# Three taps of a grouped convolution: summed in the accumulator, or shifted by small DMAs and summed in the next product

## The chip, the cores and the metric

The kernel runs on one core of a Trainium2 chip. The time is that of one execution on the device, in microseconds (us). Of the engines, TensorE multiplies matrices (PE in the profile, its weight loads PEld), VectorE (DVE) and ScalarE (ACT) work on whole tiles and can read the accumulators, GpSimd (POOL) works on tiles in the main on-chip memory, and SyncE (SP) starts DMAs. ScalarE and GpSimd can start DMAs too, each in its own row of instructions.

## The reference, cut to what matters

Two layers run one after the other on an image batch of shape (2, 128, 256, 256) in float32. The first is a group norm and a windowed attention with halo; the change leaves it alone. The second is a group norm and this convolution block, added to its input:

```python
t1 = conv(x, w1, padding=((2, 2), (0, 0)))                 # 128 -> 128 channels, 5 rows
t3 = conv(t1, w3, padding=((1, 1), (0, 0)), groups=128)    # 3 rows, per channel
xp = pad(x, columns by (2, 2))
t2 = stack([xp[..., 0:w], xp[..., 2:w + 2], xp[..., 4:w + 4]], axis=2)
t4 = einsum('nckhw,ckg->nghw', t2, w4[:, :, 0, :])         # 3 taps, 128 -> 8 channels
t5 = t4[:, None] * t3.reshape(n, 16, 8, h, w)
x = x + t5.reshape(n, 128, h, w)
```

`t4` takes each pixel and its neighbours two columns to the left and to the right, multiplies the 128 channels of each with a matrix of 128 x 8, and sums the three. Its 8 channels are then multiplied into 128 channels of `t3`, channel `ch` taking channel `ch % 8` of `t4`.

## The kernel before

The second layer is `convolutions_fast`. It goes over 64 strips `k`, 32 for each image, each of 8 rows of 256 columns, with the 128 channels in the partitions. The instructions of every engine stand in the order in which the Python code gives them (`manual_schedule`), so an engine that waits holds everything behind it.

Per strip, in the order of the code:

- `load_rows1(k + 2)` (L629) starts two loads from SyncE, L636 and L638, two strips ahead.
- `unfold(k)` (L686) makes `t4`. `g` is one accumulator bank of 128 x 512. Its four groups of 32 partitions hold two rows of the strip each, and of the 32 only 8 carry data; the weights are padded with zeros to 32 columns. For each of the three taps there are four matrix products (L692), one for each group, and the three taps are summed in the accumulator by `start=tap == 0, stop=tap == 2`. ScalarE copies the bank to `t4` (L698).
- `first_rows(k)` (L709): ScalarE copies two rows of `t1` from the strip before (L723).
- In strips 1 and 2 a step of a range check (`count_good`), and in strips 2 to 7 steps of the group norm of the second image (`norm.steps`). Some of these are small products whose result goes to bank `b3`, some are small operations on VectorE, among them L119, and one is a square root on ScalarE (L139), with its table load.
- `start_strip(k + 1)` (L666) normalises the next strip: ScalarE copies four rows that overlap (L649), VectorE does the new ones (L651).
- `vertical(k, 2)` (L727) makes the first four rows of the vertical convolution `t1`. The products `a_c`, `a_d`, `a_e`, `a_o` take one bank each, in this order, from a pool of three (`ps_a`, L618). ScalarE copies `a_c` to `both` (L737). VectorE adds `both` to `a_d` (L744, giving `c`), then `c` to `a_e` (L751) and to `a_o` (L757). ScalarE multiplies the rows with the first tap of `w3` (L762).
- `row_sums(k + 1)` (L670): a small ScalarE copy (L677) and two VectorE operations (L678, L682) for the next strip.
- `depthwise(k, 2)` (L764): two VectorE operations, L769.
- `vertical(k, 4)`: the same for the last four rows.
- `spread(k)` (L774): four products (L780) with the constant `sel` spread the 8 channels of `t4` over 128 partitions, one bank each, `b0` to `b3`. Each has 32 partitions of `t4` as its inner dimension; `sel` has a one at row `ch % 8` of each 32.
- `combine` multiplies the four banks with `t3` on VectorE (L789), with `depthwise(k, 4)` between the first two and the last two; `finish(k)` (L794) lets GpSimd start a DMA that adds the layer's input to the strip (L797), and SyncE the store (L798).

The first layer and the fallback function `tile_halo_attention_then_conv`, which does not run on these inputs, are not touched, though the fallback has functions of the same names.

Of the kernel before, what the change touches and what calls it, by code (L numbers as in the profile page):

```python
# [9 lines left out]
F32 = mybir.dt.float32  # L10
# [9 lines left out]
P = 128  # L20
W = 256
# [27 lines left out]
def host_constants():  # L49
    ident = np.eye(P, dtype=np.float32)  # L50
    gavg = np.zeros((P, P), np.float32)
    for g in range(P // 4):
        gavg[4 * g : 4 * g + 4, 4 * g : 4 * g + 4] = 0.25

    kb = np.zeros((HEADS, 32, 6, 10), np.float32)
    for c in range(10):
        kb[:, c, :, c] = 1.0
    for r in range(6):
        kb[:, 10 + r, r, :] = 1.0
    kb[:, 16, :, 6:] = NEG  # L60
    kb[:, 17, :, :4] = NEG
    flag = np.zeros((2, 4 * NPAIR * 4, 2, 4), np.float32)
    flag[0, :, 0] = 1.0
    flag[1, :, 1] = 1.0


    hot = np.zeros((2, HEADS, 16, 2, 64), np.float32)
    for key in range(64):
        j, i = divmod(key, 6)
        for e in range(2):  # L70
            if 0 <= j - 4 * e < 6:
                hot[:, :, j - 4 * e, e, key] = 1.0
            else:
                hot[:, :, 12, e, key] = NEG
            if key < 60:
                hot[:, :, 6 + i, e, key] = 1.0


    keep = np.zeros((2, HEADS, 16, 2, 2), np.float32)
    for i in range(2):  # L80
        keep[:, i::2, 0:12, i, 0] = 1.0
        keep[:, i::2, 12, i, 1] = 1.0

    sel = np.zeros((4, 32, P), np.float32)
    for ch in range(P):
        sel[:, ch % 8, ch] = 1.0
    return {
        "c_ident": ident,
        "c_sel": sel.reshape(P, P),
        "c_gavg": gavg,  # L90
        "c_kb": kb.reshape(P, 60),
        "c_flag": flag.reshape(2, 4 * NPAIR, 32),
        "c_hot": hot.reshape(P, 128),
        "c_keep": keep.reshape(P, 4),
        "c_head": np.stack([(np.arange(P) // DH % 2 == i) for i in range(2)], 1).astype(np.float32),
    }


class Norms:


    def __init__(self, nc, glob, small, gavg, ns):
        self.nc, self.glob, self.small, self.gavg, self.ns = nc, glob, small, gavg, ns
        self.done = {}
# [478 lines left out]
class Weights:  # L583


    def __init__(self, nc, io, glob):
        self.nc, self.io = nc, io
        self.w1 = glob.tile([P, 5, P], F32, tag="w1", name="w1")
        self.w3 = glob.tile([P, 3], F32, tag="w3", name="w3")
        self.w4 = glob.tile([P, 3, 32], F32, tag="w4", name="w4")  # L590
        self.sel = glob.tile([P, P], F32, tag="sel", name="sel")
        self.w1s = glob.tile([P, 6, P], F32, tag="w1s", name="w1s")

# [13 lines left out]
def convolutions_fast(tc, io, x1_d, norm, st_y, out, weights, count_good):  # L607

    nc = tc.nc
    NB, _, H, _ = io["x"].shape  # L610
    NS = H // 8
    with ExitStack() as l1:
        cst = l1.enter_context(tc.tile_pool(name="f_l1c", bufs=1))
        rawp = l1.enter_context(tc.tile_pool(name="f_raw1", bufs=6))
        tp = l1.enter_context(tc.tile_pool(name="f_t1", bufs=2))
        wk = l1.enter_context(tc.tile_pool(name="f_wk1", bufs=2))
# [4 lines left out]
        w1, w3, w4, sel, w1s = weights.w1, weights.w3, weights.w4, weights.sel, weights.w1s  # L621
# [19 lines left out]
        def normalise1(b, s, k, mean, rstd):  # L641
            cur, prev = xn[k % 2], xn[(k + 1) % 2]
            if s == 0:
                nc.gpsimd.memset(cur[:, 0:1, :], 0.0)
                nc.vector.tensor_scalar(
                    cur[:, 1:4, 2 : 2 + W], raws[b, -1][:, 5:8, :], mean, rstd, ALU.subtract, ALU.mult
                )
            else:
                nc.scalar.copy(cur[:, 0:4, :], prev[:, 8:12, :])  # L649
            n = 8 if s + 1 < NS else 5  # L650
            nc.vector.tensor_scalar(  # L651
                cur[:, 4 : 4 + n, 2 : 2 + W], raws[b, s][:, 0:n, :], mean, rstd, ALU.subtract, ALU.mult
            )
            if n < 8:
                nc.gpsimd.memset(cur[:, 4 + n : 12, :], 0.0)

        t1s, sms, dfs = {}, {}, {}

# [5 lines left out]
        def start_strip(k):  # L666
            b, s = divmod(k, NS)
            normalise1(b, s, k, *norm.done[f"y{b}"])
# [17 lines left out]
        def unfold(k):  # L686

            xt = xn[k % 2]
            pg = ps_pj.tile([P, 512], F32, tag="pj", name=f"g_{k}")
            for tap in range(3):  # L690
                for j in range(4):
                    nc.tensor.matmul(  # L692
                        pg[32 * j : 32 * j + 32, :], w4[:, tap, :],
                        xt[:, 2 * j + 1 : 2 * j + 3, 2 * tap : 2 * tap + W],
                        start=tap == 0, stop=tap == 2,
                    )
            t4 = wk.tile([P, 512], F32, tag="t4", name=f"t4_{k}")
            nc.scalar.copy(t4, pg)  # L698
            t3 = wk.tile([P, 8, W], F32, tag="t3", name=f"t3_{k}")
            y = wk.tile([P, 8, W], F32, tag="y", name=f"y_{k}")  # L700
            ts[k] = t4, t3, y
# [7 lines left out]
        def first_rows(k):  # L709

            s = k % NS
            xt = xn[k % 2]

            t1s[k] = t1 = tp.tile([P, 10, W], F32, tag="t1", name=f"t1_{k}")
            if s == 0:
                nc.gpsimd.memset(t1[:, 0:1, :], 0.0)
                top = taps(
                    f"{k}_first", 1,
                    [(w1[:, tap], xt[:, tap - 1 : tap, 2 : 2 + W]) for tap in (2, 3, 4)],
                )  # L720
                nc.scalar.copy(t1[:, 1:2, :], top)
            else:
                nc.scalar.copy(t1[:, 0:2, :], t1s[k - 1][:, 8:10, :])  # L723
            if s + 1 == NS:
                nc.gpsimd.memset(t1[:, 9:10, :], 0.0)
# [48 lines left out]
        def spread(k):  # L774

            t4 = ts[k][0]
            banks = []
            for j in range(4):
                pb = ps_b.tile([P, 512], F32, tag=f"b{j}", name=f"b_{k}_{j}")
                nc.tensor.matmul(  # L780
                    pb, sel[32 * j : 32 * j + 32, :], t4[32 * j : 32 * j + 32, :], start=True, stop=True
                )
                banks.append(pb)
            return banks
# [29 lines left out]
        with tc.manual_schedule(engines=ORDERED):  # L814
            for k in range(2):
                load_rows1(*divmod(k, NS))
            start_strip(0)
            row_sums(0)
            for k in range(NB * NS):
                more = k + 1 < NB * NS  # L820
                if k + 2 < NB * NS:
                    load_rows1(*divmod(k + 2, NS))
                unfold(k)
                first_rows(k)


                if k in (1, 2):
                    count_good[k - 1](ps_b, "b3")
                if k == 2:
                    steps = norm.steps(st_y[NB - 1], ps_b, f"y{NB - 1}", "b3")  # L830
                for _ in range({3: 1, 4: 2, 5: 2, 6: 1, 7: 1}.get(k, 0)):
                    next(steps)
                if more:
                    start_strip(k + 1)

                vertical(k, 2)
                if more:
                    row_sums(k + 1)
                depthwise(k, 2)
                vertical(k, 4)  # L840
                banks = spread(k)
                combine(k, banks, (0, 1))
                if not more:
                    finish_half(k, 0)
                depthwise(k, 4)
                combine(k, banks, (2, 3))
                if more:
                    finish(k)
                else:
                    finish_half(k, 1)  # L850
# [559 lines left out]
def lay_out(inputs):  # L1410

    c = np.ascontiguousarray
    w_qkv = np.asarray(inputs["L0_conv_W_qkv"])
    rel = np.concatenate(
        [np.asarray(inputs["L0_conv_rel_width"]).T, np.asarray(inputs["L0_conv_rel_height"]).T], axis=1
    )
    w4 = np.asarray(inputs["L1_conv_w4"])[:, :, 0, :]
    return {
        "x": c(np.asarray(inputs["x"])),
        "w_qkvT": c(w_qkv.T),  # L1420
        "w_q": c(w_qkv[:P]),
        "w_outT": c(np.asarray(inputs["L0_conv_W_out"]).T),
        "relT": c(np.tile(rel, (HEADS, 1))),
        "w1T": c(np.asarray(inputs["L1_conv_w1"])[:, :, :, 0].transpose(1, 2, 0)),
        "w3": c(np.asarray(inputs["L1_conv_w3"])[:, 0, :, 0]),
        "w4": c(np.tile(w4, (1, 1, P // w4.shape[-1]))),
        "w4g": c(np.pad(w4, ((0, 0), (0, 0), (0, 32 - w4.shape[-1])))),
        **host_constants(),
    }

# [16 lines left out]
```

## Time and profile before

| | |
|---|---|
| median of 3 runs | 3231.89 us (3228.91 to 3233.07) |
| the profiled execution | 3226.79 us |
| its span, as the profile counts | 3224.9 us |
| mean clock granted to TensorE | 0.996 of full speed |
| busy, share of the span | PE 96%, PEld 71%, DVE 81%, ACT 45%, POOL 18% |

Busy shares are means over two layers with different limits. These are the groups of the second layer's instructions that the change touches or that stand beside them, with count, busy time and the mean duration of one, and after the second bar the idle time of the engine just before them and what ended it:

```profile
L706 PE MATMUL a_e<-xm,w1s 128*128 128x512 f32 x512 | 240.7, 591 | 0.0
L762 ACT ACTIVATE t<-t,w 128x1024 f32<-128x1024 f32 x128 | 147.2, 1150 | 689.0 <-DVE t L757 689.0
L769 DVE SCALAR_TENSOR_TENSOR t<-t,w,t 128x1024 f32<-128x1024 f32 x256 | 329.9, 1289 | 7.5 <-ACT t L762 1.3
L797 POOL DMA_DIRECT2D y<-f_x x63 | 71.3, 1131 | 1025.1 <-DVE y L789 960.7
```

Matrix products overlap in time, so their durations do not add up; the distance between their starts says more. A product in float32 appears as two instructions.

### The profile page before, as it was taken

The page shows a single profiled execution, that of the slowest core. Times are in us where ns is not written, and L with a number is a line of the kernel's source. Part 1 is how long each engine was busy: PE and PEld are TensorE (multiplying, and loading weights), DVE is VectorE, ACT ScalarE, POOL GpSimd, SP SyncE. Part 2 cuts the span into 40 slices and gives each one's busy share as a digit, 9 for nine tenths or more (in the row PEclk, how much of TensorE's full clock was granted, in tenths as well). Part 3 has the DMA queues.
Part 4 walks back from the last instruction along what each step waited for, and adds up shares of the span by engine and source line. Part 5 has one row for each costly group of instructions (what it writes and reads, how often), then busy time and mean ns, then how long its engine had stood idle before and what let it go on. Part 6 is the DMA issues. An engine that isn't in the chain of part 4 may idle for free.

```text
span 3224.9 us, 117425 instructions
## 1 busy us (share of the span) xinstructions
PE 3084.4 (96%) x53030; PEld 2282.9 (71%) x53030; DVE 2611.7 (81%) x4152; ACT 1440.3 (45%) x2481; POOL 586.7 (18%) x917
## 2 busy tenths in 40 slices
PE   0799999999999999999999999989999999999998
PEld 0688898899988889988998889834444444444443
DVE  8788888888888777777777777678888898888887
ACT  0455555555555555555555555522332323233322
POOL 2222222222222222222222222100000000000001
PEclk9999999999999999999999999999999999999999
DMA  9443333333333222222222222146677767676775
GB/s 396 148 133 111 122 108 111 110 120 119 107 111 99 81 75 80 85 68 86 80 78 85 68 88 81 40 135 160 187 194 182 185 186 190 178 190 186 194 182 153
DMA packets 125116, 426.42 MB, mean 132 GB/s; under 512 B 9024, under 2 KB 75328, under 8 KB 92096
## 3 DMA queue, kind: packets, MB, share of 16 engines
q1 hardware_dynamic: 115536, 352.76, 32.2%
q0 software_dynamic: 9072, 66.06, 11.3%
q8 instruction: 420, 6.88, 0.9%
q14 instruction: 88, 0.72, 0.1%
HBM read 284.57 MB, written 134.22 MB: 130 GB/s over the span
## 4 chain that ended last, share of the span: by engine, by line
PE 76%; issue 18%; DVE 2%; POOL 2%; DMA 1%; ACT 0%; SPq 0%; POOLq 0%; DVEq 0%; ACTq 0%
PE f_pv L416 15%; PE f_pq L341 8%; PE f_s L451 8%; PE f_o L476 8%; PE f_pk L341 7%; PE f_py L341 7%; PE a_e L706 5%; PE a_o L706 5%; PE f_pa L395 4%; PE f_s L435 4%; PE g L692 3%; PE a_d L740 2%; POOL y L797 1%; PE b L780 1%; PE a_c L706 1%
## 5 line engine op out<-in xcount | busy, mean ns | idle before, releaser
L422 DVE COPY f_vt<-f_pv 64x512 f32<-64x512 f32 x512 | 354.3, 694 | 291.6 <-ACT f_vt L422 291.4
L416 PE MATMUL f_pv<-f_wqkvT,f_xn 128*128 128x128 f32 x4096 | 491.4, 278 | 0.0
L416 PEld LDWEIGHTS f_pv<-f_wqkvT,f_xn 128*128 128x128 f32 x4096 | 466.9, 192 | 8.6
L762 ACT ACTIVATE t<-t,w 128x1024 f32<-128x1024 f32 x128 | 147.2, 1150 | 689.0 <-DVE t L757 689.0
L323 POOL COPY f_xq<-f_xn 128x256 f32<-128x256 f32 x512 | 309.7, 649 | 757.8 <-DVE f_xn L309 757.8
L376 ACT ACTIVATE f_q<-f_pq,f_head 128x512 f32<-128x512 f32 x512 | 309.9, 687 | 304.2 <-PE f_pq L341 304.2
L460 ACT ACTIVATE f_p<-f_s 128x512 f32<-128x512 f32 x512 | 264.3, 603 | 404.1 <-PE f_s L451 404.0
L422 ACT COPY f_vt<-f_pv 64x512 f32<-64x512 f32 x512 | 297.4, 582 | 118.0 <-PE f_pv L416 117.8
L769 DVE SCALAR_TENSOR_TENSOR t<-t,w,t 128x1024 f32<-128x1024 f32 x256 | 329.9, 1289 | 7.5 <-ACT t L762 1.3
L451 PEld LDWEIGHTS f_s<-f_q,f_kt 64*64 64x64 f32 x16384 | 250.6, 135 | 49.3 <-issue 49.3
L341 PE MATMUL f_pq<-f_xn,f_wq_s 128*128 128x192 f32 (+2 forms) x1520 | 277.2, 330 | 3.3 <-DVE f_xn L309 2.6
L451 PE MATMUL f_s<-f_q,f_kt 64*64 64x64 f32 x16384 | 268.2, 220 | 0.0
L476 PE MATMUL f_o<-f_vt,f_p 128*32 128x66 f32 x16384 | 265.3, 223 | 0.9 <-DVE mean_x L125 0.3
L797 POOL DMA_DIRECT2D y<-f_x x63 | 71.3, 1131 | 1025.1 <-DVE y L789 960.7
L476 PEld LDWEIGHTS f_o<-f_vt,f_p 128*32 128x32 f32 x16384 | 243.2, 111 | 10.5 <-DVE f_cf L408 1.0
L341 PE MATMUL f_pk<-f_xn,f_wqkvT 128*128 128x256 f32 x1024 | 245.3, 380 | 0.0
L341 PEld LDWEIGHTS f_pq<-f_xn,f_wq_s 128*128 128x128 f32 x1520 | 232.3, 188 | 17.0 <-issue 4.2
L341 PE MATMUL f_py<-f_ot,f_woT 128*128 128x256 f32 x1024 | 241.8, 378 | 2.3 <-DVE f_ot L494 2.3
L706 PE MATMUL a_e<-xm,w1s 128*128 128x512 f32 x512 | 240.7, 591 | 0.0
L706 PE MATMUL a_o<-xm,w1s 128*128 128x512 f32 x512 | 240.5, 590 | 0.0
L300 POOL COPY f_xn<-f_xn 128x1280 f32<-128x1280 f32 x62 | 86.5, 1395 | 772.1 <-PE f_pv L416 772.1
L510 DVE TENSOR_TENSOR f_x<-f_py,f_raw 128x512 f32<-128x512 f32 x256 | 175.9, 687 | 58.7 <-PE f_py L341 50.7
(126 smaller groups left out, 4612.6 us busy)
## 6 DMA issues: line engine op xcount, KB each, us to landing
f_raw<-in_x SPq DMA_DIRECT2D x62, 1280.0 KB, 7.8
f_sx<-in_x SPq DMA_DIRECT2D x64, 1024.0 KB, 7.3
f_x<-f_x SPq DMA_DIRECT2D x128, 512.0 KB, 3.3
y<-f_x POOLq DMA_DIRECT2D x63, 1024.0 KB, 8.2
out<-y SPq DMA_DIRECT2D x63, 1024.0 KB, 4.9
raw<-f_x SPq DMA_DIRECT2D x64, 640.0 KB, 6.4
raw<-f_x SPq DMA_DIRECT2D x62, 384.0 KB, 6.9
f_raw<-in_x SPq DMA_DIRECT2D x2, 1024.0 KB, 6.9
```

The lines of the kernel that those rows point to most:

```text
L323: nc.gpsimd.tensor_copy(xq[:, t2, half].rearrange("p t r n c e -> p r t (n c) e"), cells[:, :, 16 * half : 16 * half + 16, 1 + t2 : 9 : 4, ...
L341: nc.tensor.matmul(dst[:, 32 * lo : 32 * hi], w, moving[:, lo:hi], start=True, stop=True)
L376: nc.scalar.activation(q[:, c, :, i], pq.rearrange("p (n x) -> p n x", n=NPAIR), AF.Copy, scale=head[:, i : i + 1],)
L416: nc.tensor.matmul(pv[:, P * n : P * n + P], xn[k % 2][:, r, 4 * j + n].rearrange("p c x -> p (c x)"), wvT, start=True, stop=True,)
L422: (nc.vector.tensor_copy if c else nc.scalar.copy)(vt[rows, 4 * j : 4 * j + 4, :, c, 0:32], pv[rows].rearrange("p (n h d) -> p n h d", n=4 ...
L451: nc.tensor.matmul(sc[g][n // 8][64 * c : 64 * c + 64, n % 8].rearrange("p i x -> p (i x)"), keys_k[rows, c, 48 * n : 48 * n + 64], qs[u][ ...
L460: nc.scalar.activation(pts[u][:, g, 8 * half : 8 * half + 8].rearrange("p n i x -> p (n i x)"), sc[g][half].rearrange("p n i x -> p (n i x ...
L476: nc.tensor.matmul(po[32 * h : 32 * h + 32, n - lo], p[:, h // 2, n, h % 2], vt[:, n, h], start=True, stop=True,)
L510: nc.vector.tensor_tensor(x1[:, :, c:W:2], py.rearrange("p (m t) -> p t m", t=4), raws[k][:, r:8:2, c:W:2], ALU.add,)
L706: nc.tensor.matmul(pa[:, : n * W], w, rows, start=i == 0, stop=i == len(terms) - 1)
L762: nc.scalar.activation(t3[:, j : j + 4], t1[:, j : j + 4, :], AF.Copy, scale=w3[:, 0:1])
L769: nc.vector.scalar_tensor_tensor(t3[:, j : j + 4], t1[:, j + tap : j + tap + 4, :], w3[:, tap : tap + 1], t3[:, j : j + 4], ALU.mult, ALU.add,
```

## The change

The three taps of `t4` are no longer summed in the accumulator. One set of weights holds the 8 columns of each of the three taps side by side, 24 of 32, so four products per strip give the contributions of each pixel to all three taps. ScalarE copies the bank to a tile `by_pixel`, and then starts twelve DMAs for each strip, one for each tap and group: 8 partitions, two rows of 254 or 256 columns, moved by -2, 0 or +2 columns into a tile `t4`. There are two such tiles, which take turns and are set to zero once. The products of `spread` sum over the taps, as `sel` now has a one in three places of each 32 rows. The steps of the range check and of the norm, and `start_strip` before `vertical(k, 2)`, change places: `start_strip(k + 1)` and `vertical(k, 2)` come first, the steps follow.

```diff
-    sel = np.zeros((4, 32, P), np.float32)
+    sel = np.zeros((4, 4, 8, P), np.float32)
     for ch in range(P):
-        sel[:, ch % 8, ch] = 1.0
+        sel[:, 0:3, ch % 8, ch] = 1.0
...
-        self.w4 = glob.tile([P, 3, 32], F32, tag="w4", name="w4")
+        self.w4 = glob.tile([P, 32], F32, tag="w4", name="w4")
...
+        shifted = [cst.tile([P, 2, W], F32, tag=f"t4{i}", name=f"t4_{i}") for i in range(2)]
+        for i in range(2):
+            nc.gpsimd.memset(shifted[i], 0.0)
...
             pg = ps_pj.tile([P, 512], F32, tag="pj", name=f"g_{k}")
+            for j in range(4):
+                nc.tensor.matmul(
+                    pg[32 * j : 32 * j + 32, :], w4, xt[:, 2 * j + 1 : 2 * j + 3, 2 : 2 + W],
+                    start=True, stop=True,
+                )
+            by_pixel = wk.tile([P, 2, W], F32, tag="t4", name=f"t4_{k}")
+            nc.scalar.copy(by_pixel.rearrange("p r w -> p (r w)"), pg)
+
+            t4 = shifted[k % 2]
             for tap in range(3):
+                o = 2 * tap - 2
+                lo, hi = max(0, -o), W - max(0, o)
                 for j in range(4):
-                    nc.tensor.matmul(
-                        pg[32 * j : 32 * j + 32, :], w4[:, tap, :],
-                        xt[:, 2 * j + 1 : 2 * j + 3, 2 * tap : 2 * tap + W],
-                        start=tap == 0, stop=tap == 2,
-                    )
-            t4 = wk.tile([P, 512], F32, tag="t4", name=f"t4_{k}")
-            nc.scalar.copy(t4, pg)
+                    rows = slice(32 * j + 8 * tap, 32 * j + 8 * tap + 8)
+                    nc.scalar.dma_start(t4[rows, :, lo:hi], by_pixel[rows, :, lo + o : hi + o])
...
                 nc.tensor.matmul(
-                    pb, sel[32 * j : 32 * j + 32, :], t4[32 * j : 32 * j + 32, :], start=True, stop=True
+                    pb, sel[32 * j : 32 * j + 32, :],
+                    t4[32 * j : 32 * j + 32].rearrange("p r w -> p (r w)"), start=True, stop=True,
                 )
...
                 unfold(k)
                 first_rows(k)
+                if more:
+                    start_strip(k + 1)
+
+                vertical(k, 2)
...
                 for _ in range({3: 1, 4: 2, 5: 2, 6: 1, 7: 1}.get(k, 0)):
                     next(steps)
-                if more:
-                    start_strip(k + 1)
-
-                vertical(k, 2)
                 if more:
                     row_sums(k + 1)
```

The host pads the weights accordingly (`w4.reshape(P, -1)`, 24 columns to 32).

More of the change, by code (lines that the diff above doesn't have):

```diff
@@ L1426, in lay_out @@
         "w4": c(np.tile(w4, (1, 1, P // w4.shape[-1]))),
-        "w4g": c(np.pad(w4, ((0, 0), (0, 0), (0, 32 - w4.shape[-1])))),
+        "w4g": c(np.pad(w4.reshape(P, -1), ((0, 0), (0, 8)))),
         **host_constants(),
```

## The prediction, made before the changed kernel ran

> **What bounds the kernel now.** I read the busy times by stretch first. The change lies wholly in the second layer (from about 2101 us on), so only that stretch counts. Columns after the stretch and its length are busy us with instruction counts of TensorE, its weight loads, VectorE, ScalarE, GpSimd, then granted clock, DMA share and GB/s.
> ```profile
> 2400.00:2600.00 200.00, 200.00 (x796) 91.49 (x792) 177.50 (x201) 61.23 (x95) 13.01 (x12) 1.00 0.71 186
> ```
> TensorE never rests, VectorE is at 89%, ScalarE at 31%. The accumulating load (L797) starts 59 times between 2213.6 and 3200.0 us, so a strip takes 17.0 us. VectorE works 15.1 us of that. Next, the chain of waits in order of time, for one strip (start, length, what):
> ```profile
> 2516.02 2.74 PE g L692 x24
> 2518.75 0.63 PE a_c L706 x2
> 2519.38 0.86 PE a_d L740 x4
> 2520.25 2.58 PE a_e L706 x6
> 2522.82 2.58 PE a_o L706 x6
> ...
> 2532.07 1.07 PE b L780 x8
> ```
> The whole chain of a strip is TensorE. Times below are from the strip's start (2516.02 = 0). Then ScalarE's timeline of the same strip:
> ```profile
> 2516.57 1.15 ACT L762 ACTIVATE t<-t,w 128x1024 f32<-128x1024 f32 x1 [5.53 <-DVE t L757]
> 2518.81 0.58 ACT L698 COPY t<-g 128x512 f32<-128x512 f32 x1 [1.10 <-PE g L692]
> 2519.29 0.62 ACT L723 COPY t<-t 128x512 f32<-128x512 f32 x1
> 2519.81 1.06 ACT L649 COPY xm<-xm 128x1040 f32<-128x1040 f32 x1
> 2520.78 0.37 ACT L737 COPY both<-a_c 128x256 f32<-128x256 f32 x1
> ```
> ScalarE is idle on average, but this row of four copies ends in `both`, which frees the bank that the first product of `a_o` takes: `ps_a` has three banks, `a_c`, `a_d`, `a_e` fill them, and `a_o` takes the first again. `both` ends at 5.13, `a_o` starts at 6.80: slack 1.7 us. That is the place to watch, as the twelve new DMAs are issued by ScalarE ahead of L723, L649 and L737.
>
> What does an issue cost? No DMA is issued by ScalarE in this trace. SyncE's timeline at the start has eight in a row:
> ```profile
> 1.64 0.43 SPq L172 DMA_DIRECT2D f_woT<-in_w_outT  x1
> 2.12 0.43 SPq L172 DMA_DIRECT2D f_hot<-in_c_hot  x1
> 2.59 0.43 SPq L172 DMA_DIRECT2D f_keep<-in_c_keep  x1
> 3.06 0.43 SPq L172 DMA_DIRECT2D f_head<-in_c_head  x1
> ```
> 1 KB (f_head) or 64 KB (f_woT), the spacing is 0.47 us: the price is for the instruction, not its bytes.
>
> Last, what a rest does to TensorE, from its timeline and the stretches around the normalisation step of 2191 us:
> ```profile
> 2191.45 0.38 PE L122 MATMUL pm_y<-mv_y,f_gavg 128*128 128x1 f32 x2 [3.04 <-DVE y L789]
> 2191.69 1.09 PE L706 MATMUL a_c<-sm,w1s 128*128 128x256 f32 x2
> 2192.57 1.06 PE L740 MATMUL a_d<-df,w 128*128 128x256 f32 x2
> ```
> ```profile
> 2193.00:2195.00 2.00, 2.00 (x5) 1.35 (x4) 1.29 (x2) 0.24 (x1) 0.00 (x0) 0.50 0.99 131
> ```
> After 3.04 us of rest the clock was 0.50 (the mean is 0.71 over the two us before and 0.94 over the two after, so some 3.4 us of half clock), and the work from 2191.69 to 2195.62 took 3.93 us where the strip above needs 2.15 for it (0.43 for `a_c`, 0.86 for `a_d`, 0.86 for the first third of `a_e`): 1.8 us lost. Of the three rests of this kind (3.08 us at 2149, 3.04 at 2188, 3.06 at 2210) only this one lowered the clock.
>
> **What the Trainium skill says.** "Perfetto Trace Analysis", section "DMA Instruction — HWDGE (DVE, Sync)": the recorded time of an issue runs until the sequencer is free for its next instruction, data movement not included. So 0.43 us is time in which ScalarE's later instructions wait; SyncE's spacing agrees. "DMA: Bandwidth & Descriptors", section "SWDGE vs HWDGE vs iDMA": a DMA from ScalarE is made by the same hardware as one from SyncE, so I carry SyncE's price over; no run here shows it yet. Same page, "Why a DMA increments its semaphore by 16 and not by 1": a transfer of 8 partitions runs on 8 engines, and the sequencer adds the other 8 increments itself. No trace here shows that form; it speaks for dearer issues, not cheaper. "TensorE: Matmul & The Clock Gate", section "Part 1": the array falls to half clock after an idle window of about 3.4 us and needs as long of work to recover. The trace agrees in kind (clock 0.50, up again after some 3.4 us), but once after 3.04 us already.
>
> **The change, part by part.**
>
> 1. Products `g`: 12 become 4 per strip. Each group of four runs side by side in 0.86 us, so 2.74 becomes 1.02 us: 1.72 us less for TensorE in each strip.
>
> 2. `b` keeps its form and number (1.07 us); only the rows of `sel` fill up. The copy of `g` stays (0.58 us). The two memsets run on GpSimd, 13 us busy in 200, before the first strip: nothing. One load of weights is 32 KB smaller: nothing.
>
> 3. Twelve issues on ScalarE. The first waits for the copy of `g`. That copy stands behind L762 of the strip before (ends at 1.70 in the trace, set by VectorE), so it ends near 2.2, though `g` is done at 1.02. Price of one: SyncE's spacing 0.47 for 128 rows. L514, with 512 rows, is recorded with 0.51, L798, with 128, with 0.34: 0.45 ns for a row, 0.05 us less for 8 to 16 rows. A little back for the increments: I take 0.44. Bounds: 0.33 (about the shortest issue in the trace, with no gap), 0.60 (about L275's median, 0.62). 12 x 0.44 = 5.3 us. From 2.25 they end at 7.55; L723, L649 and `both` follow in 0.52 + 0.97 + 0.37 and some 0.1 of starts, as spaced in the trace: `both` ends at 9.5. Queued behind it on ScalarE are L762, the copy of `sm` and the second `both`, and VectorE's `c`, `df` and L769 wait for these.
>
> 4. TensorE after it: `a_e` ends 4.06 us after `g`, at 5.08, then TensorE rests until 9.53. From the start of `a_o` to the next `g` the chain has 10.1 us (2505.93 to 2516.02 in the strip before). Period 9.53 + 10.1 = 19.6 us. VectorE's round, from the same `both` through `a_o`, L757, L762, `sm`, `df`, two L769, `c`, L751, L757, L762, the copy of `g` and the issues, comes to the same 19.6, so nothing pulls it in.
>
> 5. The rest is now 4.45 us, longer than the three above. I take half clock in two of three strips, at 1.8 us: 1.2 us. Bounds: none, and 1.8 in each. Period 20.8 us, 3.8 more than 17.0; over 63 strips, +239 us.
>
> 6. The landing. `b` starts at 18; the last issue is at 7.5 and small loads at the start landed in 1.9 to 2.4 us. Ten us of slack: nothing. With eight completion semaphores handed round, as the built program shows, the ninth issue of a strip waits for its first to land (3.5 us earlier: landed), and the eighth waits for the strip before's last `raw` load. That one is issued at 14.9 and lands 6.9 us later, at 21.8, which is 1.0 in a strip of 20.8 and before the eighth issue at 5.3. Hidden here, but see the rival of cheap issues.
>
> 7. Normalisation and counting steps, strips 2 to 7. Before, ScalarE's copies of `g` stand 20.2, 19.3, 21.9 and 20.2 us apart from strip 2 to 6: 81.6 against 4 x 17.0, 13.6 us lost, mostly to TensorE waiting for bank b3 until VectorE's L789 of the strip before. Behind `vertical(k, 2)` that bank is long free: gone. In exchange L119 (3.6 us) stands between L757 and L678 on VectorE, and the table load (1.3 us) ahead of the copy of `sm`, both on the round: 5 back. Net -8 us (bounds -14 and +5).
>
> Sum against the profiled execution: 3226.8 + 239 - 8 = 3458. That execution is 5.1 us under the median of the runs (3231.9), so 3463; I say 3460.
>
> **Rivals.**
>
> *The issues hold ScalarE, but the clock stays up* (two of three short rests kept it). Period 19.6: 63 x 2.6 - 8 = +156, 3388 us. At 0.33 us an issue the rest falls to 3.1 us: period 18.3, +74, 3306.
>
> *Dearer issues*: at 0.60 us the hold is 7.2, `a_o` starts at 11.5, the rest is 6.4 us and the clock falls each time: 11.5 + 10.1 + 1.8 = 23.4, 63 x 6.4 - 8 = +395, 3627. The flat 0.47 over all sizes speaks against.
>
> *Not slower*: ScalarE issues cheaply, as nothing in this trace prices its own. It decides from 9.53 - 5.3 + 12 d + 10.1 = 17.0, d = 0.22 us. With d = 0.1 the sum alone gives 15.5, VectorE's 15.1 plus its 0.44 wait for `sm` the same. But then the eighth issue meets part 6's semaphore: the load lands at 21.8, that is 21.8 less the period, and four more issues and the three copies follow, so twice the period is 21.8 + 0.5 + 2.0 + 10.1 = 34.4: 17.2 us, no gain beyond part 7. If the loads move up with the shorter strip and land 1.5 us earlier, 16.5: 63 x -0.5 - 8 = -40 us, 3192. All of SyncE's issues in the trace, at 0.32 or more, speak against.
>
> **How the numbers follow.** The hold with half clock in most strips 0.55 (its own range 3390 to 3530), the hold with full clock or slightly cheaper issues 0.25, dearer issues 0.08, cheap issues 0.12 (0.09 faster, 0.03 about equal). The range 3300 to 3560 leaves out the cheap issues and most of the dear ones. A difference under 0.2% (6.5 us) can't be told from none. Faster 0.09, same 0.03, slower 0.88.
>
> **What would show it.** ScalarE's queue with twelve issues a strip, 0.4 to 0.5 us apart, between the copy of `g` and that of the two rows of `t1` (L723 before); `a_o` waiting for `both` by some 4 us in each strip; a mean clock near 0.94 over stretches of the second layer; VectorE's share down to some 73%; strips 20 to 21 us apart. Wrong if issues stand under 0.2 us apart, if `both` comes before 6 us, or if TensorE waits at `b` for the shifted rows instead.

## The result, and the profile after

| | before | after |
|---|---|---|
| median of the runs | 3230.4 us | 3774.78 us (3768.13 to 3777.88) |
| ratio, 95% interval | | 1.1683 (1.1667 to 1.1699) |
| the profiled execution | 3226.79 us | 3777.88 us |
| its span | 3224.9 us | 3776.1 us |
| strip to strip, mean from 2400 to 3000 us | 16.94 us | 25.58 us |

The changed kernel is 17% slower. The forecast had the direction and the place, but with 3460 us only 42% of the loss, and the time lies above its range.

The busy times of a stretch, columns as in the prediction, and four lines of the page: the shares of the chain that ended last, and three groups with count, busy time, mean ns of one, and the idle time of the engine before them with what ended it.

```profile
2600.00:2800.00 200.00, 135.35 (x406) 60.74 (x405) 119.21 (x135) 40.53 (x64) 8.62 (x8) 0.84 0.50 126
```

```profile
PE 63%; ACTq 13%; DVE 8%; ACT 7%; issue 6%; DMA 2%; POOL 0%; SPq 0%; DVEq 0%; POOLq 0%
...
L715 PE MATMUL a_o<-xm,w1s 128*128 128x512 f32 x512 | 354.7, 830 | 496.1 <-ACT both L746 496.1
...
L753 DVE TENSOR_TENSOR c<-a_d,both 128x512 f32<-128x512 f32 x128 | 88.0, 688 | 391.8 <-ACT both L746 391.8
...
L732 ACT COPY t<-t 128x512 f32<-128x512 f32 x62 | 38.3, 617 | 561.2 <-DMA t<-t 561.2
```

TensorE fell from 200 us busy in 200 to 135, at a clock of 0.84, and VectorE from 177.5 to 119. Of the chain that ended last, 13% is now "ACTq", which is ScalarE's own row of DMA issues; before, it was 0%. `a_o` waited 496 us for `both`. The 561 us in front of L732 are put down to a DMA, but nothing waits there for a landing: the chain of waits of one strip shows what fills them (start, length, what; four of the twelve issues and all else up to `a_o`, without the pieces of 0.04 us between them).

```profile
2607.39 0.57 ACT t L699
2607.98 0.69 ACTq L707
...
2608.72 0.70 ACTq L707
...
2613.68 1.08 ACTq L707
...
2616.30 0.99 ACTq L707
...
2617.33 0.62 ACT t L732
2617.95 0.96 ACT xm L649
2618.91 0.28 ACT both L746
...
2619.23 4.52 PE a_o L715 x6
```

The copy of `g` ends, then twelve issues follow with gaps of 0.04 us, ten of 0.63 to 0.72 us and two of 1.08 and 0.99 in this strip. L732, the copy of `xm` and `both` come after them in the order written, and `a_o` starts 0.04 us after `both`. L732 starts 0.04 us after the last issue ends. The shortest landing measured on this queue is 1.7 us (in the run with transfers of 128 partitions, below, of 22 KB instead of 16), so L732 did not wait for it.

What the rest does to TensorE, in its timeline of two strips (start, busy time, engine, line, what, number of instructions, in brackets the idle time before and what ended it):

```profile
2439.33 3.78 PE L715 MATMUL a_o<-xm,w1s 128*128 128x512 f32 x4 [7.89 <-ACT both L746]
2442.90 1.91 PE L715 MATMUL a_o<-xm,w 128*128 128x512 f32 x2
...
2465.29 3.78 PE L715 MATMUL a_o<-xm,w1s 128*128 128x512 f32 x4 [7.66 <-ACT both L746]
2468.86 1.10 PE L715 MATMUL a_o<-xm,w 128*128 128x512 f32 x2
```

Four instructions that take 1.88 us at full clock took 3.78 us here; in the 62 strips that have such a rest (6.8 to 9.5 us) they took 3.42 to 3.78. In each second strip the next two are slow as well, 1.91 us against 1.10. The granted clock shows why they alternate (columns as above, the clock stands third from the end):

```profile
2434.89:2445.11 10.22, 5.78 (x8) 2.60 (x9) 1.64 (x3) 1.85 (x3) 0.00 (x0) 0.50 0.85 207
2445.13:2462.17 17.04, 12.50 (x46) 5.63 (x44) 13.45 (x15) 3.33 (x5) 1.08 (x1) 1.00 0.29 83
2462.19:2469.00 6.81, 3.71 (x5) 1.65 (x6) 1.39 (x2) 1.85 (x3) 0.00 (x0) 0.50 0.81 210
```

Half clock begins within the rest and lasts 10.2 and 6.8 us in turns, three and two times 3.41 us. What of it lies behind the start of `a_o` is work at half speed: the first stretch ends 5.8 us after 2439.33, which loses 2.9 us, the second 3.7 us after 2465.29, which loses 1.9.

A strip after the change in two parts, as means over ten strips from 2401 us on, beside the prediction: from the start of `g` to that of `a_o` 12.96 us (predicted 9.53), and from there to the next `g` 12.63 us, in turns some 12.1 and 13.2 (predicted 11.3, with 10.1 at full clock). Together 25.6 against 20.8.

### The profile page after: what moved, and what is told of

Same layout as the page of the kernel before. It is cut to its first block, busy times and chain, and to the rows that moved or that the text cites. A ratio compares the mean times of both kernels' runs of the same rounds, so it can differ in the third digit from the quotient of the medians.

```text
span 3776.1 us, 116400 instructions
## 1 busy us (share of the span) xinstructions
PE 3134.3 (83%) x52006; PEld 2303.5 (61%) x52006; DVE 2616.5 (69%) x4152; ACT 1438.6 (38%) x2481; POOL 582.8 (15%) x919
## 4 chain that ended last, share of the span: by engine, by line
PE 63%; ACTq 13%; DVE 8%; ACT 7%; issue 6%; DMA 2%; POOL 0%; SPq 0%; DVEq 0%; POOLq 0%
PE f_pv L416 13%; ACTq L707 13%; PE a_o L715 9%; PE f_pq L341 7%; PE f_s L451 7%; PE f_o L476 7%; PE f_pk L341 6%; PE f_py L341 6%; PE f_pa L395 4%; PE f_s L435 4%; ACT t L771 3%; DVE t L766 2%; DMA t<-t 2%; DVE t L778 2%; DVE df L685 2%
## 5 line engine op out<-in xcount | busy, mean ns | idle before, releaser
L715 PE MATMUL a_o<-xm,w1s 128*128 128x512 f32 x512 | 354.7, 830 | 496.1 <-ACT both L746 496.1
L715 PEld LDWEIGHTS a_o<-xm,w1s 128*128 128x128 f32 x512 | 122.4, 254 | 676.0 <-ACT both L746 548.4
L753 DVE TENSOR_TENSOR c<-a_d,both 128x512 f32<-128x512 f32 x128 | 88.0, 688 | 391.8 <-ACT both L746 391.8
L807 POOL DMA_DIRECT2D y<-f_x x63 | 66.8, 1061 | 1569.1 <-DVE y L799 1517.6
L732 ACT COPY t<-t 128x512 f32<-128x512 f32 x62 | 38.3, 617 | 561.2 <-DMA t<-t 561.2
L766 DVE TENSOR_TENSOR t<-a_o,c 128x512 f32<-128x512 f32 (+1 forms) x128 | 87.4, 682 | 226.9 <-PE a_o L715 226.9
```

Of the source, the lines that this page charges most:

```text
L715: nc.tensor.matmul(pa[:, : n * W], w, rows, start=i == 0, stop=i == len(terms) - 1)
```

## Experiments

Two questions were open: why one issue costs 0.70 us and not 0.44, and whether issues and clock explain the whole loss. The first four runs take the change apart.

**Without the shifting DMAs** (`t4` is the unshifted copy; the shift of the two outer taps is left out).

```diff
-                    nc.scalar.dma_start(t4[rows, :, lo:hi], by_pixel[rows, :, lo + o : hi + o])
+            t4 = by_pixel
```

> The changed kernel without the twelve DMAs; the products of spread read the unshifted tile, so the shift of two taps by two columns is left out. If the hold of ScalarE by the issues is what costs the time, strips fall to what TensorE and VectorE need: 15.3 us of products, 15.1 us of VectorE work and its 0.44 us wait, so about 15.6 us a strip and 3120 to 3140 us in all. If the smaller products or the new order cost time themselves, it stays above 3200.

Measured: 3192.47 us, ratio 0.9882 (0.9867 to 0.9897), clock 0.993. So the loss comes with the DMAs and not with the products or the order of the steps; but the gain of the shorter products is smaller than expected, in neither of the two ranges. Strips are 16.63 us apart, where TensorE has 15.2 us of work (16.94 less the 1.72 of the products). The waits between 2400 and 3000 us have a line that is small in the kernel before, with 5.6 us in 7 cases (who, for what, us, times, longest):

```profile
DVE xm L651 <- DMA raw<-f_x: 21.7, 23, 2.2
```

In 23 of 36 strips VectorE waited for the next rows, `raw`. SyncE issues these loads behind the store of the strip before, which waits for the accumulating DMA. A later run follows this up.

**Twelve issues of 128 partitions** (the same number from ScalarE at the same place, each 43 columns wide; the rows are copied unshifted, so the shift of the outer taps is left out).

```diff
-                    nc.scalar.dma_start(t4[rows, :, lo:hi], by_pixel[rows, :, lo + o : hi + o])
+            for i in range(12):
+                cols = slice(43 * i, min(43 * i + 43, 512))
+                nc.scalar.dma_start(flat_to[:, cols], flat_from[:, cols])
```

> Twelve issues per strip from ScalarE as in the changed kernel, but each moves all 128 partitions of some 43 columns, unshifted (the shift is left out). The issues of the changed kernel were recorded with 0.63 to 0.72 us, SyncE's with 0.34 to 0.43. If their shape [...] makes them dear, they fall to about 0.43 us here, the hold to 5.6 us and the time to some 3430 to 3500 us. If ScalarE issues at a dearer rate than SyncE whatever the shape, they stay near 0.7 us and the time near 3775 us.

Measured: 3758.93 us, ratio 1.1639 (1.1618 to 1.166). ScalarE's timeline in a strip:

```profile
2602.13 8.65 ACTq L706 DMA_DIRECT2D t<-t  x12
```

The median of one issue is 0.61 us against 0.70, which is neither of the two expectations: the small shape is part of the price, but a small part. The hold, from the first issue to the end of the twelfth, falls only from 8.97 to 8.71 us as the mean of all 64 strips, since more issues took over 0.85 us (19% against 6%); 63 times 0.26 us are the 16 us by which the time fell.

**The twelve DMAs from SyncE**, ahead of the next loads, and the store of the strip before behind both, so that neither waits for the store.

```diff
-                    nc.scalar.dma_start(t4[rows, :, lo:hi], by_pixel[rows, :, lo + o : hi + o])
+                    nc.sync.dma_start(t4[rows, :, lo:hi], by_pixel[rows, :, lo + o : hi + o])
...
+                unfold(k)
                 if k + 2 < NB * NS:
                     load_rows1(*divmod(k + 2, NS))
-                unfold(k)
+                if k > 0:
+                    store(k - 1)
```

> The changed kernel with its twelve shifting DMAs issued by SyncE, ahead of the loads and of the store of the strip before. Shape as cause: SyncE's issues of 8 partitions are recorded with 0.63 to 0.72 us too. ScalarE as cause: 0.35 to 0.43 us. Either way ScalarE is free, both comes early, TensorE does not rest and keeps its clock: 15.6 to 16 us a strip, 3130 to 3160 us, faster than the kernel before by 2 to 3%. If the landing of the shifted rows becomes the wait, TensorE stands at the products b and the time is above 3200.

Measured: 3165.25 us, ratio 0.98 (0.9785 to 0.9815): 2% faster than the kernel before, and 5 us above the range expected. SyncE's timeline, and below it some of TensorE's in the same strip:

```profile
2604.06 10.29 SPq L707 DMA_DIRECT2D t<-t  x12
...
2614.87 0.59 SPq L636 DMA_DIRECT2D raw<-f_x  x1
```

```profile
2605.58 1.88 PE L715 MATMUL a_e<-xm,w1s 128*128 128x512 f32 x4
2607.30 1.88 PE L715 MATMUL a_o<-xm,w1s 128*128 128x512 f32 x4
...
2616.71 1.76 PE L789 MATMUL b<-t,sel 32*128 32x512 f32 x8
```

Twelve issues take SyncE 10.29 us here (median of one 0.69, against 0.70 from ScalarE), then come the loads. So an issue is not dearer on ScalarE, and the DMAs themselves, which are the same twelve, are not what costs the time. The price of the issues has not gone either; it stands in a row where no compute instruction is queued behind it. TensorE runs from `a_e` to `a_o` without a rest, and the strips are 16.11 us apart. The landing now touches the path: `b` takes 1.76 us instead of 1.14, and in 31 strips of the whole run its products waited for the rows in `t`, 15.6 us in all (their weight loads 30.8).

**Only the new order of the steps**, with the old products and no DMAs: `start_strip(k + 1)` and `vertical(k, 2)` before the steps of check and norm.

```diff
                 first_rows(k)
+                if more:
+                    start_strip(k + 1)
+                vertical(k, 2)
                 ...
-                if more:
-                    start_strip(k + 1)
-
-                vertical(k, 2)
                 if more:
                     row_sums(k + 1)
```

> The kernel before with only the new order of the norm's and the check's steps behind vertical(k, 2). The prediction put this at -8 us (bounds -14 and +5): the three rests of TensorE of 3 us each go, L119 with 3.6 us and the table load with 1.3 us move onto VectorE's and ScalarE's path. The rival is that the rests only move: within 3 us of the kernel before.

Measured: 3217.53 us, ratio 0.9963 (0.9949 to 0.9976), 12 us less. ScalarE's copies of `g` in the strips of the steps:

```profile
2152.85 0.59 ACT L698 COPY t<-g 128x512 f32<-128x512 f32 x1 [1.08 <-PE g L692]
...
2170.05 0.58 ACT L698 COPY t<-g 128x512 f32<-128x512 f32 x1 [1.41 <-PE g L692]
...
2188.89 0.57 ACT L698 COPY t<-g 128x512 f32<-128x512 f32 x1
...
2205.87 0.58 ACT L698 COPY t<-g 128x512 f32<-128x512 f32 x1 [0.79 <-PE g L692]
...
2222.99 0.58 ACT L698 COPY t<-g 128x512 f32<-128x512 f32 x1 [1.32 <-PE g L692]
```

From strip 2 to 6 they are 17.2, 18.8, 17.0 and 17.1 us apart, where the prediction read 20.2, 19.3, 21.9 and 20.2 in the kernel before: 11.4 us less over four strips, which is the gain.

The next four runs test the sum of issues and clock, follow the two late loads, and try fewer issues.

**Six issues instead of twelve** (the shifted rows of a strip's last two groups are left out and stay zero).

```diff
-                for j in range(4):
+                for j in range(2):
                     rows = slice(32 * j + 8 * tap, 32 * j + 8 * tap + 8)
```

> The changed kernel with the shifting DMAs of the first two groups only: six issues on ScalarE in each strip instead of twelve. Left out: the shifted rows of the last two groups of a strip, which stay zero in the multiplication. Theory, the price of each issue adds up: six at 0.74 us are 4.4 us, `both` ends near 8.6, TensorE rests some 3.5 us; period 18.7 at full clock, 20.5 at half clock in every strip: 3320 to 3440 us, in the place where the prediction put twelve issues. Rival, a fixed cost of having such DMAs at all (their wait, their semaphores, the tiles) makes the loss: it stays above 3650.

Measured: 3438.32 us, ratio 1.0649 (1.0632 to 1.0665). ScalarE's timeline in a strip, then TensorE's `g` and `a_o` in two other strips:

```profile
2608.61 4.39 ACTq L707 DMA_DIRECT2D t<-t  x6
...
2614.52 0.36 ACT L746 COPY both<-a_c 128x256 f32<-128x256 f32 x1
```

```profile
2401.53 1.08 PE L694 MATMUL g<-xm,w 128*32 128x512 f32 x8
...
2410.14 3.57 PE L715 MATMUL a_o<-xm,w1s 128*128 128x512 f32 x4 [3.46 <-ACT both L746]
...
2422.01 1.08 PE L694 MATMUL g<-xm,w 128*32 128x512 f32 x8
...
2430.61 3.57 PE L715 MATMUL a_o<-xm,w1s 128*128 128x512 f32 x4 [3.46 <-ACT both L746]
```

Six issues hold ScalarE for 4.39 us, 0.73 each. From `g` to `a_o` it is 8.61 us, from `a_o` to the next `g` 11.87, 1.8 more than at full clock, in strip after strip. The clock is low for 3.41 us, from within the rest on:

```profile
2430.44:2433.84 3.40, 3.23 (x4) 1.51 (x5) 1.38 (x2) 0.12 (x1) 0.00 (x0) 0.50 0.91 188
```

The clock fell in 60 of the 62 strips with a rest over 2 us (3.46 at the median); after one of 3.12 us and one of 3.48 us, at 2797.61, it stayed at full. The loss is by the issue: six fewer give 336 us back, 5.2 us in each strip (25.58 less 20.36), of which 4.5 are issues (8.9 less 4.4) and some 0.7 is half clock. A fixed cost per strip as the main cause is ruled out. With a hold of 4.4 instead of 5.3 us the prediction's own sum gives some 3410 us with half clock in two of three strips and 3448 with half clock in each; measured 3438. So the steps after the price of an issue were sound, but for "two of three strips". That the time lies so near the forecast 3460 is in part luck: a shorter hold and more half clock offset each other.

**Keeping TensorE busy through the rest**: nine products into a spare bank that nobody reads, between `a_e` and `a_o`.

```diff
+            if warm:
+                pw = ps_pj.tile([P, 512], F32, tag="pj", name=f"warm_{k}")
+                for i in range(warm):
+                    nc.tensor.matmul(pw, w1[:, 0], rows(0), start=True, stop=True)
```

> The changed kernel with nine products that nobody reads, on TensorE between `a_e` and `a_o` of the first half of each strip, 0.86 us each, in place of its rest of some 8 us. They lengthen nothing if `both` comes as late as before. Theory, half clock after the rest is time lost in addition to the rest, 1.8 to 2.4 us in every strip: 3775 falls by 63 x 1.8 to 2.4, to 3620 to 3660, and the mean clock of the second layer goes up to 0.97 or more. Rival, VectorE and ScalarE set the period by themselves and TensorE's slower work lies beside theirs: 3750 to 3790.

Measured: 3669.13 us, ratio 1.1364 (1.1346 to 1.1381), mean clock from 2400 to 3000 us 0.99; 9 us above the range of the theory and far below the rival's. One strip:

```profile
2607.58 7.90 PE L764 MATMUL warm<-xm,w 128*128 128x512 f32 x18
2615.82 1.98 PE L715 MATMUL a_o<-xm,w1s 128*128 128x512 f32 x4 [0.34 <-ACT both L746]
...
2626.11 1.08 PE L694 MATMUL g<-xm,w 128*32 128x512 f32 x8
```

After the eighteen filling instructions `a_o` takes 1.98 us instead of 3.78, and the next `g` comes 10.29 us after `a_o` instead of 12.63. So of the 544 us that the change costs, 106 are half clock that work without use can buy back. It is a floor for that part, as the filling itself ends later than `both` in some strips; by the granted clock of the kernel after, half clock loses some 2.3 us a strip. The rest of the loss stays; the runs with six issues and with the issues on SyncE put it down to the hold.

**Without the shifting DMAs, loads ahead of the store** (shift left out as in the first run).

```diff
                     load_rows1(*divmod(k + 2, NS))
+                if k > 0:
+                    store(k - 1)
```

> The run without shifting DMAs (left out: the shift of the two outer taps) with the two loads of a strip issued ahead of the store of the strip before, where the store stood first and waits for the accumulating DMA. Theory, the late landing of these loads held the shorter strips: 3120 to 3140 us, ratio 0.966 to 0.972. Rival, the loads were not the limit (VectorE's round through `both` and `c` was): within 0.4% of the run with the store first, 3180 to 3205.

Measured: 3145.23 us, ratio 0.9742 (0.9727 to 0.9757). That is 47 us below the first run, 5 us above the range of the theory and far below the rival's. The line of VectorE's normalisation (duration min/median/max, first and last start, shapes; below it the idle time before it in the whole run, and how often):

```profile
L651 DVE TENSOR_SCALAR xm<-raw,mean_y,rstd_y x64: 1336/1339/1597, 2107.2 to 3102.4; 128x2048 f32<-128x2048 f32 x62, 128x1280 f32<-128x1280 f32 x2
...
  DMA raw<-f_x: 3.6, 1
```

One wait of 3.6 us is left, where the same view of the first run has 39.7 us in 40 cases. So the late loads were what held most of the gain back in the strips of 16.63 us; in the kernel before, with 16.94, moving them gains nothing (last run).

**Five DMAs in a strip, from SyncE.** ScalarE copies the middle tap in place; the 8-column blocks of the weights stand in turned order in every second group, so that two neighbouring groups share a DMA of 16 partitions; the source has zero borders, so every DMA has one form. Loads ahead of the store, as above.

```diff
+            nc.scalar.copy(t4, rows2)
+            for lo, hi, tap in ((0, 8, 0), (24, 40, 2), (56, 72, 0), (88, 104, 2), (120, 128, 0)):
+                nc.sync.dma_start(t4[lo:hi], by_pixel[lo:hi, :, 2 * tap : 2 * tap + W])
```

> Five shifting DMAs in each strip, issued by SyncE ahead of the loads: the middle tap is copied by ScalarE in place (a second copy of `g`, 0.5 us), the columns of the weights alternate so that neighbouring groups share a DMA of 16 partitions, and the zero borders stand in the source. Five issues of 0.7 us are 3.7 us instead of nine, so the rows land 5 us earlier and `b` waits for nothing: 3110 to 3150 us, or ratio 0.963 to 0.975, against 3165 with twelve from SyncE. Rival, VectorE's own 15.1 us and its round with ScalarE set the strip already, and the extra copy lengthens it: 3160 to 3200.

Measured: 3144.41 us, ratio 0.974 (0.9726 to 0.9753), the fastest kernel of this study that does the whole computation. SyncE's row and the busy times of a stretch:

```profile
2608.52 3.76 SPq L705 DMA_DIRECT2D t<-t4p  x5
```

```profile
2600.00:2800.00 200.00, 197.60 (x666) 89.24 (x665) 188.24 (x215) 68.62 (x113) 14.63 (x15) 1.00 0.80 208
```

This equals the run that makes no shift at all (3145.23), so five DMAs on this row cost nothing that can be seen. Strips are 15.84 us apart. The chain of waits of one (start, length, what) is TensorE again, but for one operation of VectorE:

```profile
2723.41 2.59 PE a_o L713 x6
2726.00 0.70 DVE t L758
...
2726.74 1.13 PE a_d L747 x4
```

TensorE does not start the second `a_d` before L758 is done, 0.70 us a strip. With TensorE at 197.6 us busy in 200 and VectorE at 188, both are nearly full.

The last two runs price an issue and the loads' place, each by itself.

**The price of an issue by itself.** Behind the end of the kernel before, sets of six DMAs each, from SyncE and from ScalarE.

```diff
+            for engine in (nc.sync, nc.scalar):
+                for i in range(6):
+                    engine.dma_start(to[:, i, 0:128], io["c_sel"])
+                for i in range(6):
+                    engine.dma_start(to[:, i, 128:171], src[:, 0:43])
...
```

> The kernel before, with rows of DMAs at its end that change nothing of its work, in sets of six, once from SyncE and once from ScalarE: from DRAM into 128 partitions x 128 columns; within on-chip memory 128 x 43 columns; within on-chip memory 8 partitions x two rows of 254 columns (the form of the change), 8 x 512 and 16 x 512 in one row; from DRAM into 8 x 512. Its total time is not of interest. Theory, a DMA within on-chip memory is dearer to issue than one from DRAM, whatever its shape: 0.43 to 0.48 us for both sets from DRAM, 0.58 to 0.70 for all sets within. Rival a, the few partitions make it dear: 0.60 to 0.70 for the sets of 8 and 16 partitions, from DRAM too, and 0.43 to 0.50 for both of 128. Rival b, no set differs when issued alone, all within 0.40 to 0.50: then 0.70 came from issuing beside other traffic. ScalarE against SyncE: within 0.05 us in each set under the theory.

The durations by line, min/median/max in ns, of four of the sets on ScalarE's row (ACTq; `in_c_sel` and `in_w1T` lie in DRAM, `price_src` on chip):

```profile
L859 ACTq DMA_DIRECT2D price_to<-in_c_sel x6: 334/388/443, 3252.8 to 3255.4; - x6
...
L861 ACTq DMA_DIRECT2D price_to<-price_src x6: 499/608/612, 3255.9 to 3259.1; - x6
...
L863 ACTq DMA_DIRECT2D price_to<-price_src x6: 693/696/1359, 3259.8 to 3264.3; - x6
...
L872 ACTq DMA_DIRECT2D price_to<-in_w1T x6: 287/306/510, 3272.9 to 3274.8; - x6
```

| transfer | ScalarE, median us | SyncE, median us |
|---|---|---|
| DRAM, 8 partitions x 512 | 0.31 | 0.29 |
| DRAM, 128 x 128 (two sets) | 0.39, 0.44 | 0.43, 0.35 |
| on chip, 16 x 512 | 0.60 | 0.59 |
| on chip, 128 x 43 | 0.61 | 0.60 |
| on chip, 8 x 512 | 0.63 | 0.62 |
| on chip, 8 x two rows of 254 | 0.70 | 0.69 |

Rival a and rival b both fall: 8 partitions from DRAM are the cheapest of all, and the sets on chip are dear without other traffic. Among these small transfers, an issue whose two ends both lie on chip costs 0.2 to 0.3 us more than one from DRAM. (A store to DRAM, L798 in the kernel before, took 0.34.) That DRAM at one end makes an issue cheap in general is not shown: the larger load L638 of the kernel before took 0.91 us at the median. The two rows of 254 add 0.07 to one row of 512. The theory's 0.58 to 0.70 for the sets on chip came true; those from DRAM came out below its 0.43 to 0.48 with 8 partitions and in two of the four sets with 128. ScalarE and SyncE differ by at most 0.04 us, apart from the second DRAM set of 128 (0.09), where SyncE's row also shows waits.

**Only the loads ahead of the store**, in the kernel before.

> The kernel before with one alteration: the two loads of a strip stand ahead of the store of the strip before in SyncE's row. Theory, TensorE sets the strip there and the loads are early enough: within 0.3% of the kernel before, so the gain of 2% with twelve issues from SyncE is that of the shorter products and not of the loads' place. Rival, the loads' place was worth something by itself: 3170 to 3210 us.

Measured: 3227.12 us, ratio 0.9997 (0.9991 to 1.0004). Nothing, as TensorE sets the strip there. So the loads' place gave nothing by itself to the versions from SyncE: their 2% and 2.6% are put down to the shorter products and the 12 us of the moved steps, and the loads' place lets the products' gain through.

## Why the prediction fell short

The prediction named the right mechanism: twelve issues hold ScalarE, `both` comes late, TensorE rests, and its clock falls. Two terms of its sum were too small, by 3.6 and 1.3 us a strip.

- **Step 3, the price of one issue**, "I take 0.44", bounds 0.33 and 0.60: this is what failed. Measured 0.70 recorded and 0.04 between, and twelve took 8.9 us (8.73 to 9.40, as the mean of 24 strips) instead of 5.3: 3.6 us a strip. The true value lay outside both bounds. All of SyncE's issues that the step leaned on have DRAM at one end, and "the flat 0.47 over all sizes" is that of the eight issues at the start, of that one kind. The change issues another kind, on chip to on chip, which the trace of before does not have once. Nor was the price flat in the rest of that trace: besides L275's 0.62 us it has 62 issues of L638, the smaller of the two loads of a strip, which the step left out (0.44 to 1.98 us). With 0.91 us at the median they alone would have put the upper bound above 0.60. The step carried the price over to another engine, which was right ("DMA: Bandwidth & Descriptors", section "SWDGE vs HWDGE vs iDMA"; the two differ by 0.01 us here in the form of the change), and did not ask about the other end of the transfer. A small part is the shape: step 3 took 0.05 us off for fewer rows; between on-chip transfers fewer rows gave nothing back, and the two-row form cost 0.07 more.
- **Step 5, half clock**, "two of three strips, at 1.8 us: 1.2 us", upper bound 1.8: measured 2.5 us (12.63 less 10.1), in every strip, in turns about 2.0 and 3.1. With a rest of 3.46 us (six issues) it is 1.8 in nearly every strip; with 8 us it is more. "TensorE: Matmul & The Clock Gate", section "Part 1", says that the window of activity runs freely, so that the number of slow products varies with its phase. The granted clock agrees, and by itself accounts for 1.9 and 2.9 us: half clock came in stretches of 3.41, 6.8 and 10.2 us, with 17.1 us of full clock between. So a loss per rest is not one number: it is half of what such a stretch has left when the work resumes. The strips keep step with the stretches, most of them 20.48 us apart with six issues (3.41 + 17.07) and 51.1 for two strips with twelve (6.83 + 17.07 + 10.24 + 17.07 = 51.2); whether the clock sets this distance or the two only happen to fit was not tested.
- With both terms put right the rest of the working holds: `a_o` would start at 2.25 + 8.9 + 2.0 = 13.1 us, measured 12.96, and the period is 13.1 + 10.1 + 2.5 = 25.7, measured 25.58 (its 2.5 is taken from the same trace, so this part agrees by construction). Over 63 strips at +8.7 us and the step of -8, that makes 3767 us; the profiled execution took 3778. Most of what is left is that the first strip is held too, 64 in all. The rival "dearer issues" was this case, worked out at 0.60 us, and its chance of 0.08 was too low.
- **Step 1**, the products: right in size (1.01 us from `g` to `a_c` in the trace after), and in the two versions without the hold and with early loads, 84 and 85 us faster, worth some 72 us beside the 12 of the steps. That is 1.1 us a strip of 1.72, as 0.70 us of VectorE (L758 of the run with five DMAs, the addition of `c` to `a_e`) then stands in the chain. **Step 2**: right, `b` kept its 1.07 us.
- **Step 4**, the path to `both` and to the end of the strip: right, by the two parts of a strip with six issues (8.61 us against 2.25 + 4.4 + 2.0 = 8.65).
- **Step 6**, the landing: right for this change; `b` waited for no DMA. The completion semaphores added nothing that the trace shows (17 ns in each strip). From SyncE with twelve issues, in a strip of 16 us, the landing does come up to `b`.
- **Step 7**, the moved steps: -8 predicted, -12 measured alone (the steps of the check stand in strips 1 and 2, those of the norm in 3 to 7). Within the changed kernel strips 1 to 8 were 26.4 us apart instead of 25.6, so some 6 us of it were lost again to the longer round.

What stays open: why an issue is dearer when both ends lie on chip, and why some take 0.9 to 1.3 us. For these the traces have a clue. In the strip shown SyncE issued nothing at that time, but GpSimd had started its accumulating DMA (L807) at 2611.80, 1.9 us before the first of the two. Of the 44 issues over 0.85 us in the kernel after, 43 began 1.9 to 5.1 us after such a start, and of the 371 that began more than 10 us after one not a single issue was so long. With six issues, which are over by then, only the first of all 384 was. So the traffic of that DMA goes with the long issues; no run here takes it away to test it, and one issue of 1.36 us in the price run has no such DMA near it.

## What to carry to other kernels

Price a new DMA by a row of the same kind, both ends and the form included; if the trace has no such row, the bounds must be wide, or the price measured first, which takes a few instructions behind a kernel. A DMA's issue is an instruction of the engine that starts it: put it in a row where no compute waits behind it, and merge many small ones into few, since the price is mostly by the instruction. When a stage gets shorter, look at once at what was just in time before; here loads behind a store took 47 of 84 us.

## What the runs showed that was not expected

- An issue from on-chip memory to on-chip memory (16 to 32 KB) took 0.59 to 0.70 us, one from DRAM (16 or 64 KB) 0.29 to 0.44, on both engines, as medians of six. ScalarE's next instruction started 0.04 us after the recorded end of an issue.
- A rest of 3.46 us lowered TensorE's clock in 60 of 62 strips at a cost of 1.8 us, one of 3.48 us did not, and one of 8 us cost 2.0 and 3.1 us in turns: in these strips half clock came in stretches of one, two or three times 3.41 us.
- Products without use in place of the rest gave 106 us back, 1.7 us a strip.
